# A macaron layer on one core: the first unit's row maxima moved ahead, and the first batch's stores shared by two DMA queues

## The chip, the cores and the metric

The kernel runs on one core of a Trainium2 chip. The metric is device time in microseconds (us), the median of three runs. A core has five engines that each work through their own instructions in order: TensorE (PE in the profile; PEld is its weight load), VectorE (DVE), ScalarE (ACT), GpSimd (POOL) and SyncE (SP). DMAs are issued by an engine's instruction stream, here by SyncE and ScalarE; a DMA that has to wait for data holds up everything behind it on the engine that issues it. Engines wait for one another by semaphores. PSUM is the memory that TensorE writes to.

## The reference

Half a mixture-of-experts step, causal attention with 16 heads of 16, and the other half step, each on the normalised input and added to it. The shapes are 8 batches of 1024 tokens of 256 values.

```python
x = x + 0.5 * _L0_ffn_ref(_layernorm(x), gate_w, w1, b1, w2, b2)
x = x + _L0_attn_ref(_layernorm(x), Wq, bq, Wkv, bkv, Wo, bo)
x = x + 0.5 * _L0_ffn_ref(_layernorm(x), gate_w, w1, b1, w2, b2)
# in attention
dots = jnp.einsum('bhid,bhjd->bhij', q * scale, k)
dots = jnp.where(causal, MASK_VAL, dots)
out = jnp.einsum('bhij,bhjd->bhid', softmax(dots), v)
# in the feed-forward part: an expert counts only if it got at most `cap` tokens
keep = counts <= cap
valid = keep[a_e]
```

An expert that is chosen by more tokens than its capacity is dropped as a whole. The kernel first computes the gates and the attention as if no expert were kept, counts the choices, and only where an expert is kept after all does it run the code for experts (`tc.If` at the end). With these inputs that code does not run: what is timed is the attention, with both gates.

## The kernel before

**Units.** `attention` works in 32 units, `u` from 0 to 31: 8 batches `b` of 4 groups `g` of 4 heads (NG is 4). For each unit there are two kinds of step, 18 of each.

- *M steps* (`m_steps`): matmuls `sm<-qk` give scores with queries on the partitions, a matmul with `masked` and `before_k` adds the causal mask, and VectorE reduces each PSUM pair to row maxima (`mx<-sm`). `done` is the number of the last step that belongs to the first half of the queries. Then `settle` takes the maximum over pieces, splits its negative into a high and a low part (`mneg`), and turns it (`mside`); `send` writes it to DRAM (`rows<-mside`) and reads it back as rows (`neg<-rows`), once for each half.
- *E steps* (`e_steps`): `sc<-neg,take_m` puts the negative maxima into PSUM, `sc<-qk` adds the scores with keys on the partitions, ScalarE takes the exponential (`pT<-sc`), GpSimd zeroes what lies past the diagonal, and `pav<-pT,vaug` multiplies by the values. An E step needs the maxima of its half.

**Work of a batch**, done in pieces between those steps: `enter` (transposes `pta`, copied to `xnT` by ScalarE), `project(b, gp)` (queries and keys of 8 heads, `pq`), `values_of` (`pv`, copied to `vaug`, with the gate's logits), and later `leave` (output projection `px`, residual, second gate). `project` makes of each 128x512 piece a `whole`, its high part `high` (rounded, by ScalarE) and its low part `low` (by GpSimd), and stores four copies in DRAM (`parts<-high`, `parts<-low`): t = 0 for queries, 1 for keys, c the four copies. `fetch(u)` reads a unit's queries and keys from there (`qk<-parts`) with four DMAs. All of these DMAs are on SyncE's queue.

**Order.** The source's order is kept on each engine (`Lane` ties every instruction to the one before it on its engine). In the main loop `step` runs one M or E step, starts DMAs that are due after a lag counted in steps (`start`, `due`), takes up to `small` pieces of `side` (a queue of VectorE and GpSimd work such as `prepare`, `settle`, `gate_first`, `biased_late`), and every `every` steps takes about `rate` pieces of `work` (a queue of TensorE work). M steps run three ahead of the E steps' unit. Units of the first batch use the same `rate`, 17/12 every 3 steps, as the later ones; `u = -1` runs only the 18 M steps of unit 0.

**The start.** `read(0)` and `read(1)` load two batches; `weights` is a generator (`turning`) that loads and transposes the weights in stages, with `pt_gate`, `pt_w`, `pt_wg`, `pt_b` as its PSUM tiles. `prepare_first` and `normed` normalise batch 0 (`xn_a`), `enter(0)` and `project(0, 0)` follow, half a batch at a time with a `fetch` after each half. Then the rest of `turning`, `values_of(0)`, `prepare(1)` (the statistics and first four tiles of batch 1), memsets, the fetch of unit 1, and the main loop, with `project(0, 1)` as its first work and `biased_late(0)` and `gate_first(0)` in `side`.

Of the kernel before, what the change touches and what calls it, by code (L numbers as in the profile page):

```python
# [10 lines left out]
F32 = mybir.dt.float32  # L11
# [9 lines left out]
P = 128  # L21
# [8 lines left out]
def macaron_kernel(  # L30
# [16 lines left out]
    nc = tc.nc  # L47
# [84 lines left out]
    nc.vector.tensor_copy(take_m, rows.to_broadcast([P, P]))  # L132

    wqT = const.tile([P, DC, D], F32, name="wqT")
    wkT = const.tile([P, DC, D], F32, name="wkT")
# [466 lines left out]
    def attention(run_no, src, dst, gate0, logits, tally):  # L602
# [4 lines left out]
        with stack:  # L607
# [76 lines left out]
            def normed(b, jj):  # L684
                mv, ve, rstd = lns[b]
                for j in (2 * jj, 2 * jj + 1):
                    xn = xns[b, j] = norm.tile([P, D], F32, tag="xn", name=f"xn_a{b}_{j}", bufs=4)
                    ln_apply(xn, xbs[b], j, mv, rstd[:, j : j + 1])
                    yield
                if b:  # L690
                    biased(b, jj)

            coming = {}
# [28 lines left out]
            def prepare_first():  # L722
                st, mv = ln_tiles("a0", "a")
                ve = norm.tile([P, TB], F32, tag="vea", name="ve_a0")
                rstd = norm.tile([P, TB], F32, tag="rstda", name="rstd_a0")
                lns[0] = (mv, ve, rstd)
                for n in (slice(0, TB // 2), slice(TB // 2, TB)):
                    for j in range(TB)[n]:
                        ln_stats(xbs[0], j, st, mv)
                    on.gpsimd.tensor_scalar(ve[:, n], mv[:, n, 1], EPS, None, ALU.add)  # L730
                    on.gpsimd.tensor_tensor(rstd[:, n], ve[:, n], half[:, n], ALU.pow)

            def enter(b):
                xnT = xnTs[b] = ap.tile([P, DC, S], F32, tag="xnT", name=f"xnT{b}", bufs=1)
# [22 lines left out]
            def project(b, gp):  # L757
                xnT = xnTs[b]
                parts = parts_d[b, gp] = passing.tile([2, 8, 4, HD, S], F32, tag=f"parts{gp}", name=f"parts{b}_{gp}")
                for s0 in range(0, S, 512):  # L760
                    for t, (wT, bT, scale) in enumerate(((wqT, bqT, QSCALE), (wkT, bkT, 1.0))):
                        pq = bank(f"pq{b}_{gp}_{s0}_{t}")
                        for o in (0, 256):
                            for c in range(DC):
                                product(
                                    pq[:, o : o + 256],
                                    wT[:, c, gp * P : (gp + 1) * P],
                                    xnT[:, c, s0 + o : s0 + o + 256],
                                    start=(c == 0),
                                    stop=(c == DC - 1),  # L770
                                )
# [12 lines left out]


# [62 lines left out]
            def m_steps(u):  # L848
# [56 lines left out]
                def settle(hf):  # L905
                    mx = ap.tile([P, 4, 2, 2], F32, tag="mxr", name=f"mxr{u}_{hf}")
                    on.vector.tensor_reduce(
                        mx.rearrange("p x b a -> p x a b"),
                        mx_tiles[u % 3][hf].rearrange("p h r (a b) s -> p (h r) a b s", a=2),
                        AX.X,  # L910
                        ALU.max,
                    )
                    yield
                    mx = mx.rearrange("p x b a -> p x (b a)")
                    neg = ap.tile([P, 4, 2, 4], F32R, tag="mneg", name=f"mneg{u}_{hf}")
                    high, low = neg[:, :, 0], neg[:, :, 1]
                    on.vector.tensor_scalar(high, mx, -1.0, None, ALU.mult)
                    yield
                    on.vector.scalar_tensor_tensor(
                        low.bitcast(F32), mx, -1.0, high.bitcast(F32), ALU.mult, ALU.subtract  # L920
                    )
                    yield
                    turned = ap.tile([P, 32], F32, tag="mside", name=f"mside{u}_{hf}")
                    on.vector.transpose(turned, neg.bitcast(F32).rearrange("p x c i -> p (x c i)"))
                    start(send(hf, turned), 0)
                    yield

                def send(hf, turned):
                    rows = passing.tile([8, 512], F32, tag="rows", name=f"rows{u}_{hf}")
                    on.sync.dma_start(out=rows.rearrange("c (i s q) -> s c i q", i=4, s=4), in_=turned)  # L930
                    yield 6
                    for h in range(2):
                        on.sync.dma_start(
                            out=negs[u % 2][hf][64 * h : 64 * h + 2, :, :512].bitcast(F32),
                            in_=rows[4 * h : 4 * h + 4].rearrange("(r c) s -> c r s", c=2),
                        )
# [271 lines left out]
            next(turning, None)  # L1208
            next(turning, None)
            drain(read(1))  # L1210
            for t in (vaugs[0], *mx_tiles[0]):
                on.gpsimd.memset(t, 1.0 if t is vaugs[0] else -3.0e38)
# [7 lines left out]
            for jj in range(2, 4):  # L1220
                drain(normed(0, jj))
            projecting = project(0, 0)
            for _ in range(8):
                next(projecting)
            drain(fetch(0, 0, 512))
            drain(entering)
# [5 lines left out]
            for t in (vaugs[1], *mx_tiles[1], *mx_tiles[2]):  # L1232
                on.gpsimd.memset(t, 1.0 if t is vaugs[1] else -3.0e38)
            for pair_of in negs:
                for t in pair_of:
                    on.gpsimd.memset(t.bitcast(F32), 0.0)
# [48 lines left out]
            def maxima():  # L1285
                v, k = divmod(stream[0], 18)
                if v == NU:
                    return
                if k == 0:
                    units[v] = m_steps(v)  # L1290
                steps, settle, done = units[v]
                steps[k]()
                if k == max(done, 8) or k == 17:
                    side.appendleft(settle(int(k == 17)))
                    urgent[0] = 4
                if k == 17:
                    units.pop(v)
                stream[0] += 1

            for u in range(-1, NU):  # L1300
                b, g = divmod(u, NG)
                rate, every = 17 / 12, FILLS
                if u < 0:
                    pass
                elif g == 0:
                    spare[0] = False
                    if b + 1 < B:
# [1 line left out]
                        if b:  # L1309
                            work.append(mixed(leave(b - 1), project(b + 1, 1)))  # L1310
                        else:
                            work.append(project(b + 1, 1))
                        work.append(values_of(b + 1))
                    if b:
                        start(divide(b - 1, 1, 0), 4)
                        after[u - 1, 1] = divide(b - 1, 1, 1)
                        side.append(gate_first(b))
                elif g == 1 and b + 1 == B:
                    work.append(leave(b - 1))
                elif g == 2:  # L1320
                    if b == 0:
                        start(read(2), 40)
# [107 lines left out]
```

## Time and profile before

| | before |
| --- | --- |
| median of 3 runs | 1207.94 us (1207.55 to 1210.71) |
| profiled execution, own time | 1207.5 us |
| its span in the profile | 1205.5 us |
| mean granted TensorE clock | 0.978 of full |
| VectorE busy with `mx<-sm` | 684.7 us, 576 of 1215 ns |
| ScalarE busy with `pT<-sc` | 573.0 us, 576 of 1022 ns |
| `parts<-high` and `parts<-low` | 128 DMAs each, 256 KB each, all on SyncE's queue |
| `qk<-parts` | 124 DMAs on SyncE's queue |

The profile shows one execution. Its busy times are shares of the whole span; in a kernel of 32 like units a stage that happens once is a small share of each, so the timeline and the chain of waits of that stage have to be read. The chain goes back from a late instruction, at each step to what released it. In the timeline a line is a run of like instructions: start, length, engine, operation, out<-in, count, and in brackets the idle time before it with what ended it. "SPq" and "ACTq" lines are DMA issues of SyncE and ScalarE; their length is that of the issuing, not of the transfer. "issue" as a releaser means that the profile shows no cause. The granted clock is TensorE's, as a share of full speed.

### The profile page before, as it was taken

The page shows a single profiled execution, that of the slowest core. Times are in us where ns is not written, and L with a number is a line of the kernel's source. Part 1 is how long each engine was busy: PE and PEld are TensorE (multiplying, and loading weights), DVE is VectorE, ACT ScalarE, POOL GpSimd, SP SyncE. Part 2 cuts the span into 40 slices and gives each one's busy share as a digit, 9 for nine tenths or more (in the row PEclk, how much of TensorE's full clock was granted, in tenths as well). Part 3 has the DMA queues.
Part 4 walks back from the last instruction along what each step waited for, and adds up shares of the span by engine and source line. Part 5 has one row for each costly group of instructions (what it writes and reads, how often), then busy time and mean ns, then how long its engine had stood idle before and what let it go on. Part 6 is the DMA issues. An engine that isn't in the chain of part 4 may idle for free.

```text
span 1205.5 us, 36314 instructions
## 1 busy us (share of the span) xinstructions
PE 1138.4 (94%) x15178; PEld 663.1 (55%) x15178; DVE 935.2 (78%) x1652; ACT 735.6 (61%) x955; POOL 433.8 (36%) x772
## 2 busy tenths in 40 slices
PE   6789899999999999999999999999999999999983
PEld 4445555655556555655556555565556555555542
DVE  2687558887788877988788877888789888798834
ACT  3236656766666666665666656566666666665671
POOL 4633313543333423532235433333235322232331
PEclk9879999999999999999999999999999999999997
DMA  5644654354554646455563645546564555543211
GB/s 178 222 168 141 209 173 128 111 196 153 171 185 154 198 159 190 143 172 177 157 201 113 207 153 168 169 155 202 160 181 150 176 174 177 155 136 109 63 42 39
DMA packets 108517, 190.25 MB, mean 158 GB/s; under 512 B 24752, under 2 KB 42296, under 8 KB 108344
## 3 DMA queue, kind: packets, MB, share of 16 engines
q1 hardware_dynamic: 104952, 185.59, 47.8%
q8 instruction: 122, 2.00, 0.7%
q10 hardware_dynamic: 3392, 2.24, 0.6%
q14 instruction: 51, 0.42, 0.1%
HBM read 94.50 MB, written 93.31 MB: 156 GB/s over the span
## 4 chain that ended last, share of the span: by engine, by line
PE 76%; DVE 13%; DMA 5%; issue 1%; ACT 1%; POOL 1%; SPq 1%; POOLq 0%; ACTq 0%; DVEq 0%
PE sc L626 22%; PE pav L626 21%; PE sm L626 15%; PE pq L626 8%; DVE mx L626 8%; PE px L626 4%; PE pv L626 4%; PE pta L626 2%; DVE st_a L626 1%; DMA few<-sums 1%; DMA neg<-rows 1%; DMA rows<-mside 1%; SPq L626 1%; DVE mv_a L626 1%; DMA qk<-parts 1%
## 5 line engine op out<-in xcount | busy, mean ns | idle before, releaser
L626 DVE TENSOR_REDUCE mx<-sm 128x2 f32<-128x1024 f32 (+2 forms) x576 | 684.7, 1215 | 161.6 <-PE sm L626 159.9
L626 ACT ACTIVATE pT<-sc 128x1024 f32<-128x1024 f32 x576 | 573.0, 1022 | 309.6 <-PE sc L626 297.9
L626 PE MATMUL pav<-pT,vaug 128*32 128x256 f32 (+3 forms) x4608 | 329.7, 387 | 2.0 <-ACT att L626 1.4
L626 POOL TENSOR_SCALAR_AFFINE_SELECT pT<-pT 128x256 f32<-128x256 f32 (+1 forms) x448 | 191.0, 443 | 297.2 <-ACT pT L626 290.4
L626 PE MATMUL sm<-qk 64*128 64x512 f32 (+3 forms) x1536 | 266.2, 384 | 17.4 <-DVE mx L626 8.4
L626 PE MATMUL sc<-neg,take_m 64*128 64x512 f32 x1152 | 263.7, 454 | 16.6 <-DVE mx L626 8.9
L626 PE MATMUL sc<-qk 64*128 64x512 f32 (+3 forms) x1536 | 228.7, 334 | 0.0
L626 PEld LDWEIGHTS sm<-qk 64*128 64x128 f32 x1536 | 140.7, 187 | 120.4 <-issue 51.9
L626 POOL TENSOR_TENSOR low<-whole,high 128x512 f32<-128x512 f32 x64 | 82.0, 1282 | 311.3 <-ACT high L626 302.5
L626 PEld LDWEIGHTS pav<-pT,vaug 128*32 128x32 f32 x4608 | 113.7, 109 | 108.0 <-issue 52.2
L626 PEld LDWEIGHTS sc<-neg,take_m 64*128 64x128 f32 x1152 | 109.4, 186 | 106.8 <-issue 53.6
L626 PEld LDWEIGHTS sc<-qk 64*128 64x128 f32 x1536 | 146.2, 186 | 16.3
L626 PE MATMUL sm<-masked,before_k 64*128 64x128 bf16 (+1 forms) x1280 | 86.3, 213 | 0.0
L626 PE MATMUL pq<-xnT,wqT 128*32 128x256 f32 x1024 | 76.3, 391 | 0.5 <-ACT xnT L626 0.5
L626 PE MATMUL px<-woT,on 128*32 128x264 f32 x1024 | 76.5, 387 | 0.2 <-ACT on L626 0.2
L626 PE MATMUL pq<-xnT,wkT 128*32 128x256 f32 x1024 | 73.2, 395 | 0.0
L626 PE MATMUL pv<-wvT,xnT 128*32 128x264 f32 x1024 | 72.3, 390 | 0.0
L626 PEld LDWEIGHTS <-before_k 64*128 64x128 bf16 x1280 | 37.9, 96 | 43.1 <-issue 26.6
L626 POOL TENSOR_TENSOR x_a<-x_a,bo_all 128x512 f32<-128x512 f32 x32 | 41.6, 1304 | 28.1 <-DVE xn_a L626 28.1
L626 PEld LDWEIGHTS pq<-xnT,wqT 128*32 128x32 f32 x1024 | 34.0, 112 | 31.8 <-issue 13.9
L626 DVE TENSOR_TENSOR x_a<-px,x_a 128x256 f32<-128x256 f32 x64 | 26.2, 410 | 31.2 <-PE px L626 30.6
L626 PEld LDWEIGHTS px<-woT,on 128*32 128x32 f32 x1024 | 34.7, 110 | 26.6 <-issue 9.8
(131 smaller groups left out, 741.4 us busy)
## 6 DMA issues: line engine op xcount, KB each, us to landing
qk<-parts SPq DMA_DIRECT2D x124, 512.0 KB
parts<-high SPq DMA_DIRECT2D x128, 256.0 KB
parts<-low SPq DMA_DIRECT2D x128, 256.0 KB
sums<-att SPq DMA_DIRECT2D x62, 256.0 KB
out_dram<-x_a SPq DMA_DIRECT2D x16, 512.0 KB
on<-sums SPq DMA_DIRECT2D x30, 256.0 KB
rs<-inv SPq DMA_DIRECT2D x30, 256.0 KB
x_a<-in_L_attn_x_dram SPq DMA_DIRECT2D x13, 512.0 KB
```

Source lines behind the costliest of these rows:

```text
L626: i = call(*args, **kwargs)
```

## The change

Three things change together.

1. *The start is put in another order.* Batch 0 is normalised two tiles at a time as soon as two tiles have their statistics (`some`); the `take_m` cast moves behind it. `fetch(1)` and the statistics of batch 1 come right behind the fetches of unit 0, and `values_of(0)` becomes work of the main loop, ahead of `project(0, 1)`. So the M steps of unit 0 follow the weights directly. The loop at `u = -1` takes work after every step, 16/5 pieces in the first five steps and 16/13 in the others. The first half's maxima of unit 0 are settled right behind the step `done`.
2. *Queues.* In batch 0 ScalarE issues the stores of `high` (but for the first copy of the first half's queries and keys, which SyncE keeps), and for unit 0 also `rows` and `neg`, with other lags. The stores of `low` stay with SyncE.
3. *The first batch's fill.* Units 0 to 3 take 13/12 pieces instead of 17/12, `values_of(1)` and `project(1, 1)` are mixed, `gate_first(0)` and `biased_late(0)` enter `side` in unit 0's turn, and the bias additions of batch 1 come as `biased_late(1)` in unit 1's turn instead of beside its normalisation.

The steps themselves and the number of matmuls, copies and DMAs are as before, and nothing is changed for batches from 2 on.

```diff
@@ prepare_first
-                for n in (slice(0, TB // 2), slice(TB // 2, TB)):
-                    for j in range(TB)[n]:
+                def some(j0, j1):
+                    for j in range(j0, j1):
                         ln_stats(xbs[0], j, st, mv)
+                    n = slice(j0, j1)
                     on.gpsimd.tensor_scalar(ve[:, n], mv[:, n, 1], EPS, None, ALU.add)
                     on.gpsimd.tensor_tensor(rstd[:, n], ve[:, n], half[:, n], ALU.pow)
+                for t in (vaugs[0], *mx_tiles[0]):
+                    on.gpsimd.memset(t, 1.0 if t is vaugs[0] else -3.0e38)
+                some(0, 2)
+                some(2, 4)
+                drain(normed(0, 0))
+                next(turning, None)
+                drain(normed(0, 1))
+                on.vector.tensor_copy(take_m, rows.to_broadcast([P, P]))
+                some(4, 8)
@@ project
-                            on.sync.dma_start(out=parts[t, :, c, :, s0 : s0 + 512], in_=part.bitcast(F32))
+                            queue = on.scalar if part is high and (b or gp or s0 or c) and not b else on.sync
+                            queue.dma_start(out=parts[t, :, c, :, s0 : s0 + 512], in_=part.bitcast(F32))
@@ settle, send
-                    start(send(hf, turned), 0)
+                    start(send(hf, turned), 0 if u else 2)
+                    queue = on.sync if u else on.scalar
-                    on.sync.dma_start(out=rows.rearrange("c (i s q) -> s c i q", i=4, s=4), in_=turned)
-                    yield 6
+                    queue.dma_start(out=rows.rearrange("c (i s q) -> s c i q", i=4, s=4), in_=turned)
+                    yield 6 if u else 4
@@ the start
-            for jj in range(2):
-                drain(normed(0, jj))
-            next(turning, None)
             entering = enter(0)
...
             drain(fetch(0, 512, 512))
+            drain(fetch(1))
+            preparing = prepare(1)
+            for _ in range(TB + 1):
+                next(preparing)
...
             drain(turning)
-            drain(values_of(0))
-            drain(prepare(1))
...
-            drain(fetch(1))
-            work = deque([project(0, 1)])
-            side += [biased_late(0), gate_first(0)]
+            work = deque([values_of(0), project(0, 1)])
+            side.append(preparing)
@@ the main loop
-                if k == max(done, 8) or k == 17:
+                if k == (max(done, 8) if v else done) or k == 17:
-                rate, every = 17 / 12, FILLS
+                rate, every = (17 if b else 13) / 12, FILLS
-                            work.append(project(b + 1, 1))
-                        work.append(values_of(b + 1))
+                            work.append(mixed(values_of(b + 1), project(b + 1, 1)))
+                        if b:
+                            work.append(values_of(b + 1))
-                        side.append(gate_first(b))
+                    side.append(gate_first(b))
+                    if not b:
+                        side.append(biased_late(b))
+                elif g == 1 and b == 0:
+                    side.append(biased_late(1))
-                        step(maxima, 2, 4 if n < 5 else 4 / 3, 1)
+                        step(maxima, 1, 16 / 5 if n < 5 else 16 / 13, 1)
```

More of the change, by code (lines that the diff above doesn't have):

```diff
@@ L131, in macaron_kernel @@
     take_m = const.tile([P, P], F32R, name="take_m")
-    nc.vector.tensor_copy(take_m, rows.to_broadcast([P, P]))
     wqT = const.tile([P, DC, D], F32, name="wqT")
@@ L689, in normed @@
                     yield
-                if b:
+                if b > 1:
                     biased(b, jj)
@@ L924, in settle @@
                     on.vector.transpose(turned, neg.bitcast(F32).rearrange("p x c i -> p (x c i)"))
-                    start(send(hf, turned), 0)
+                    start(send(hf, turned), 0 if u else 2)
                     yield
                 def send(hf, turned):
+                    queue = on.sync if u else on.scalar
                     rows = passing.tile([8, 512], F32, tag="rows", name=f"rows{u}_{hf}")
-                    on.sync.dma_start(out=rows.rearrange("c (i s q) -> s c i q", i=4, s=4), in_=turned)
-                    yield 6
+                    queue.dma_start(out=rows.rearrange("c (i s q) -> s c i q", i=4, s=4), in_=turned)
+                    yield 6 if u else 4
                     for h in range(2):
-                        on.sync.dma_start(
+                        queue.dma_start(
                             out=negs[u % 2][hf][64 * h : 64 * h + 2, :, :512].bitcast(F32),
@@ L1210, in attention @@
             drain(read(1))
-            for t in (vaugs[0], *mx_tiles[0]):
-                on.gpsimd.memset(t, 1.0 if t is vaugs[0] else -3.0e38)
             prepare_first()
-            for jj in range(2):
-                drain(normed(0, jj))
-            next(turning, None)
             entering = enter(0)
@@ L1219, in attention @@
             next(entering)
-            for jj in range(2, 4):
-                drain(normed(0, jj))
             projecting = project(0, 0)
@@ L1225, in attention @@
             drain(fetch(0, 0, 512))
+            for jj in range(2, 4):
+                drain(normed(0, jj))
             drain(entering)
@@ L1228, in attention @@
             drain(fetch(0, 512, 512))
-            drain(turning)
-            drain(values_of(0))
-            drain(prepare(1))
[L1232 to L1236, printed above, removed]
-            drain(fetch(1))
-            work = deque([project(0, 1)])
-            side += [biased_late(0), gate_first(0)]
+            drain(fetch(1))
+            preparing = prepare(1)
+            for _ in range(TB + 1):
+                next(preparing)
+            for k in range(2):
+                for t in negs[k]:
+                    on.gpsimd.memset(t.bitcast(F32), 0.0)
+                for t in mx_tiles[k + 1]:
+                    on.gpsimd.memset(t, -3.0e38)
+            on.gpsimd.memset(vaugs[1], 1.0)
+            drain(turning)
+            work = deque([values_of(0), project(0, 1)])
+            side.append(preparing)
             timed = []
```

## The prediction

> **What bounds the kernel now.** I read the page first. TensorE is busy for 94% of the span, but slices 1, 2 and 6 of 40 (30 us each) have low digits, and so has the last. The change edits only the start and the first batch, so slices 1 to 8 matter.
>
> ```profile
> PE 1138.4 (94%) x15178; PEld 663.1 (55%) x15178; DVE 935.2 (78%) x1652; ACT 735.6 (61%) x955; POOL 433.8 (36%) x772
> PE   6789899999999999999999999999999999999983
> PEclk9879999999999999999999999999999999999997
> ```
>
> Next the chain of waits, from 12 to 78 us: what held back the first score matmul (`sc`, at 76.49). Columns: start, length, what.
>
> ```profile
> 19.68 5.62 DMA parts<-high
> 32.27 7.95 PE pv L626 x128
> 42.22 1.68 POOL rstd_a L626
> 43.92 2.33 DVE xn_a L626 x4
> 46.24 1.14 DVE mx L626
> 71.36 4.99 DMA neg<-rows
> 76.49 0.84 PE sc L626 x4
> ```
>
> All eight value tiles (8 us) run before the first maximum; then VectorE, in order, first normalises batch 1 (`xn_a`, waiting for GpSimd's `rstd_a`). Eighteen maxima of 1.2 us follow, from 46.16 to 72.98, and the row of maxima still has to travel through DRAM (`rows`, `neg`).
>
> Then the timeline of SyncE's queue, one line of TensorE's timeline, and busy times by stretch (columns there: PE, PEld, DVE, ACT, POOL busy, TensorE clock, DMA share, GB/s).
>
> ```profile
> 21.25 2.80 SPq L626 DMA_DIRECT2D parts<-high  x2
> 24.15 2.52 SPq L626 DMA_DIRECT2D parts<-low  x2
> 26.84 6.48 SPq L626 DMA_DIRECT2D qk<-parts  x4
> 42.95 9.33 SPq L626 DMA_DIRECT2D qk<-parts  x8
> 139.27 0.55 SPq L626 DMA_DIRECT2D neg<-rows  x2
> 143.28 1.19 SPq L626 DMA_DIRECT2D qk<-parts  x1
> 152.87 0.80 PE L626 MATMUL sm<-qk 64*128 64x512 f32 x2 [5.75 <-issue]
> ```
>
> ```profile
> 4.00:6.00 2.00, 1.09 (x4) 0.72 (x4) 1.37 (x5) 0.29 (x2) 2.00 (x4) 1.00 1.09 376
> 24.00:26.00 2.00, 0.66 (x4) 0.42 (x4) 0.00 (x0) 1.22 (x4) 0.85 (x1) 1.00 0.52 196
> 62.00:64.00 2.00, 0.80 (x2) 0.29 (x2) 2.00 (x3) 0.47 (x1) 1.27 (x1) 0.50 0.50 170
> 204.00:212.00 8.00, 6.58 (x68) 3.41 (x71) 7.83 (x16) 4.06 (x4) 1.93 (x2) 1.00 0.58 191
> ```
>
> While only SyncE's queue writes `parts`, the DMA engines are half busy (0.52) at 196 GB/s; an issue that took 0.58 us takes 1.2 to 1.4, the time of 256 KB at that rate (1.34). With two queues at work (4 to 6 us) they moved 376 GB/s. At 147 us everything stops for 5.75 us: unit 3's `sm` wants the `qk` issued at 143.28, behind a backlog of writes.
>
> Where the 18 scores of each unit begin, counted off TensorE's timeline: 76.49, 114.44, 154.74, 189.26, 219.40. So units 0 to 3 took 37.95, 40.30, 34.52 and 30.14 us, together 142.9. Unit 3 has no projection work left and waits for maxima (2.1 us) while unit 1 and 2 are crowded. The next batches take 139.5 and 139.1 though they also run `leave`.
>
> **The change, part by part.** *Up to the first maximum.* Tiles 0 to 3 are normalised some 2 us earlier, but ScalarE still issues its loads until 11.43, and its copy moves only from 11.86 to about 11.45: -0.4. Of the batch's 16 high stores 14 go to ScalarE at 0.58 us each. The first two fall where ScalarE idled 0.57 us; the four of the second half put 2.3 us ahead of the weight copies, less the 0.8 us that the fourth `high` waited for a buffer: the last weight copy goes from 26.54 to about 28.2, `pt_b` ends near 34.0 instead of 32.27, and the first `sm` runs there (now 40.09). Its data: six writes instead of eight on SyncE's queue, 2 x 1.34 + 0.5 us earlier, so the last lands near 28.5 instead of 31.7, and the four fetches by 32.5. If ScalarE's issues were stretched like SyncE's to 1.4 us, the start is 37. First maximum at 34.7 instead of 46.16. VectorE does batch 1's 16 statistics (4.6 us, 33.0 to 37.6 now) before, while it waits anyway; were its x late, they cost up to those 4.6.
>
> *The five masked steps.* TensorE now weaves all value tiles in: 8 x 1.00 (7.97 above), plus five `sm` of 0.45 to 0.65 with masks (2.8; the timeline at 40.09 and 42.85), plus about 1.2 while the clock is still half (in the trace it rose 4 us after `pt_b` began): 34.0 + 12 = 46. VectorE needs 6 for its five and idles.
>
> *The other thirteen.* TensorE: 6.2 for the `sm` (eight plain at 0.42, five masked as before), 7.7 for the four projections (1.93 each), 13.9; VectorE: 13 x 1.19 + 0.35 for an `xn`, 15.8. Coupled step by step I take 17, plus 0.8 for settling (0.21 + 0.17 + 0.17 + 0.21 where GpSimd is quiet; the two 1.2 us `mneg` of the trace lie beside GpSimd's bias additions, which move later) and one maximum of the next unit that frees the PSUM pair: 46.4 + 17 + 0.8 + 1.2 = 65.5, say 66. The second half's keys: four low writes end near 36 and four fetches bring them by 41, before 46. So the scores start at 66 instead of 76.49: **-10.5**. Bounds: 62 (VectorE never waits) and 77 (TensorE at half clock, 13.9 x 2 = 27.8 instead of 17).
>
> *The maxima's own DMAs* leave a backlogged queue (rows issued 4.1 us after `mside`). The first half's arrive long before use. For the second, ScalarE itself now waits for `rows` ahead of its second exponential: landing took 4.9 us (77.15 to 82.07) to 7.7 (131.62 to 139.27) behind a backlog; about 4 us of other work lies between, so **+1** (0 to 4). Behind it stand the exponentials, and behind them the PSUM pairs.
>
> *The batch's fill.* 13 items per unit instead of 17, with values and second projection woven, fill unit 3 as well. A full unit takes 34.45 with 17 items (units 5 to 7), so 13 cost four quarter projections less (4 x 0.48): 32.5. Units 1 and 2 at 32.6, unit 3 with 12 items 32.4, unit 0 37.95 - 1.9 = 36: 133.6 instead of 142.9, **-9.3**; as the crowded queue may keep a little, I take **-8**. Against this from the other side: a later batch, 139.3, less `leave` (8 tiles of the shape of `pv`, 8.0), plus the 3.4 that unit 0 loses at its slow start (clock 0.50 from 78 to 80 us, 0.76 to 90), is 134.7. Bounds: -2 (the stall of 5.75 and its cold restart stay) and -10.
>
> *At nothing:* `take_m`, the memsets, bias additions and gate choice of batch 0 (VectorE was 6.3 to 7.5 of 10 us busy in unit 0; GpSimd less). Were VectorE full there, the 15 gate operations of 0.2 us would cost 3.
>
> The profiled execution took 1207.5 (span 1205.5), the median is 1207.94. -10.5 + 1 - 8 = -17.5 gives 1190.4; I say **1190**.
>
> **A rule against it.** "DMA: Bandwidth & Descriptors", Rules for kernel authors, in the Trainium skill: spreading DMAs over several engines doesn't help bandwidth, since all share the same 16 DMA engines. The rows above disagree in part: one queue left half of them idle. By the rule 4 MB of writes and 2 MB of reads go at 196 GB/s from 17.5, the second half's keys come near 49, the scores start 3 us later, and the sum would be 1193.
> "TensorE: Matmul & The Clock Gate", A second HAM failure mode, warns that short idling between PSUM-paced groups swings the clock. No row shows it at 82% busy (204 to 212: clock 1.00). By the rule the thirteen steps take 27.8 and the sum would be 1201.
>
> **Rivals.**
> - *The moved work slows the maxima* (15%): the clock drops to 0.50, as from 57 to 71 us now. For: it was lost when TensorE was half idle (0.90 of 2 us at 54). Against: 82% busy kept it. Scores start at 74, gain 2.5 + 8 - 1: 1198.
> - *SyncE's backlog stays* (10%): batch 1's parts are still on SyncE, with the same four writes ahead of the fourth `qk`. Against: only one group of writes now stands between the fetches, where two did. Gain 10.5 - 1 + 2: 1196.
> - *Slower* (9%): TensorE is at half clock for the whole stretch from 34 us to the first score, and on through unit 0. The stretch holds 8.0 of values, 9.0 of `sm`, 7.7 of projections and 2.6 of the next unit's `sm` and transposes, 27.3 us at full clock, 54.6 at half: scores at 88.6, 12 late; unit 0's 20 us of M and E work at half for another 5 beyond today's: +17 - 8 + 1, 1218. It decides once scores start after 87 (76.5 + 8 - 1 + 3.6). Against: continuous work raised the clock within 5 us (32 to 34, 71).
> - *No change* (6%): part of that, scores at about 85.
>
> **How the numbers follow.** Forecast 60%: 1190, by its own bounds 1184 to 1196. The two middle rivals (25%) lie at 1196 to 1198, so 1182 to 1200 leaves out the last two cases and a little. 0.3% (3.6 us) is about what a measurement of this kernel can tell from no change. Faster: 60 + 25 = 85%; same 6%; slower 9%.
>
> **What would show it.** Right: first maximum at 34 to 35; first `sc` near 66; no stop of 5 us near 147; units 0 to 3 at 36, 33, 33, 32; DMA above 250 GB/s between 20 and 28. Wrong: first `sm` waiting for `qk` past 36; clock 0.5 after 50; ScalarE waiting for `rows`; a gap at the start of unit 2 or 4. The later batches must keep 138 to 142 each; if they change, the forecast is wrong for a reason not in it.

## The result, and the profile after

| | before | after |
| --- | --- | --- |
| median in the comparison | 1206.29 us (6 runs) | 1222.01 us (1219.36 to 1224.23, 6 runs) |
| ratio to before | | 1.0128, 95% interval 1.0101 to 1.0155 |
| profiled execution: span, mean clock | 1205.5 us, 0.978 | 1220.6 us, 0.977 |
| first `sm`; first `sc` | 40.09; 76.49 | 43.49; 74.13 |
| units 0 to 3 | 38.0, 40.3, 34.5, 30.1 | 46.4, 36.4, 32.0, 32.4 |
| start of unit 4 | 219.4 | 221.4 |
| batches 1 to 6 | 839.1 | 849.5 |
| unit 28 to the end | 147.0 | 149.7 |

The change made the kernel slower by 1.3%, where 1190 us had been forecast. A unit is counted, here and below, from the first `sc<-neg` of one unit to that of the next on TensorE's timeline. So 2.0 us of the loss are there when unit 4 starts; 13.1 come later, in batches whose source the change does not touch.

The page's first two parts after the change (busy time by engine, then the busy share in 40 slices):

```profile
PE 1142.4 (94%) x15178; PEld 664.9 (54%) x15178; DVE 935.6 (77%) x1652; ACT 734.7 (60%) x955; POOL 434.3 (36%) x774
PE   5869999999999999999999999999999999999983
PEclk9789999999999999999999999999999999999997
```

The work is the same (15178 matmuls). A slice is 30 us. TensorE lost in slice 1 (6 to 5) and in slice 3, from 60 to 90 us (8 to 6), and won in slice 2 (7 to 8) and slice 5, where the stop at 147 had been (8 to 9).

The chain of waits after, a choice of its pieces between 19 and 90 us (start, length, what):

```profile
19.00 8.28 DMA parts<-low
27.43 7.83 DMA qk<-parts
35.33 0.58 ACTq L625
37.04 1.12 PE pt_w L625 x4
43.56 0.86 PE sm L625 x5
54.58 1.24 DVE mx L625
69.70 9.24 DMA parts<-high
79.01 8.90 DMA rows<-mside
88.61 1.02 ACT pT L625
```

Before, this stretch went over VectorE and SyncE. Now it goes twice from a DMA through a DMA issue of ScalarE (ACTq) to ScalarE's own work. ScalarE's timeline shows what stood in its stream:

```profile
24.65 5.03 ACTq L625 DMA_DIRECT2D parts<-high  x2
29.78 0.69 ACT L625 ACTIVATE whole<-pq,bkT 128x512 f32<-128x512 f32 x1 [5.16 <-DMA parts<-high]
35.33 1.44 ACTq L625 DMA_DIRECT2D parts<-high  x2
36.81 0.17 ACT L625 COPY wvT<-pt_gate 128x16 f32<-128x16 f32 x1 [5.70 <-DMA parts<-high]
79.01 0.54 ACTq L625 DMA_DIRECT2D rows<-mside  x1
79.60 0.59 ACT L625 COPY xnT<-pta 128x512 f32<-128x512 f32 x1 [6.07 <-DMA parts<-high]
87.99 0.57 ACTq L625 DMA_DIRECT2D neg<-rows  x2
88.61 1.02 ACT L625 ACTIVATE pT<-sc 128x1024 f32<-128x1024 f32 x1 [7.35 <-DMA neg<-rows]
```

From the start of one issue of `high` to the end of the next passed 5.03 us, and `whole`, which stands behind them, came after 5.16 us of idling. Two more hold back `wvT` by 5.70, though that copy needs no DMA. Near 80 us `xnT` stands for 6.07 us behind two stores and `rows`, and the second exponential behind the issue of `neg` for 7.35. TensorE's timeline shows these waits arriving (its first two lines and the last), beside the first `sm` and the first `sc`:

```profile
30.52 1.11 PE L625 MATMUL pt_w<-ident,wsb 128*128 128x128 f32 x4 [5.42 <-ACT whole L625]
37.04 1.12 PE L625 MATMUL pt_w<-ident,wsb 128*128 128x128 f32 x4 [5.40 <-ACT wvT L625]
43.49 0.79 PE L625 MATMUL sm<-qk 64*128 64x512 f32 x2
74.13 0.50 PE L625 MATMUL sc<-neg,take_m 64*128 64x512 f32 x2 [0.43 <-DVE mx L625]
81.16 0.80 PE L625 MATMUL sc<-neg,take_m 64*128 64x512 f32 x2 [5.21 <-ACT pT L625]
```

Why does an issue wait at all? In the built program the DMAs of SyncE and ScalarE take eight completion semaphores in turn, whichever of the two issues them, so an issue also waits until the DMA that had its semaphore before has landed. In the chain that is a `qk<-parts` of SyncE's at 27.43, ended at 35.26, which let ScalarE's issue go at 35.33. The other waits were for older stores of ScalarE's own: the second of the two issues from 24.65 on came at 29.09, when the store of 19.95 had landed (29.07), and `rows`, whose data was ready at 72.97, at 79.01, when the store of 69.70 had (78.94). In the trace each of the 14 issues by itself took 0.58 to 1.76 us; the rest of the 5.03 was waiting. `neg` in turn waited until `rows` had landed, 8.90 us after its issue. So ScalarE went at the pace of the stores, those of both queues. "DMA: Bandwidth & Descriptors", Anatomy of one DMA (a section on GpSimd's path), in the Trainium skill, says that a wait for a semaphore happens on the sequencer that issues the DMA, ahead of dispatch; these rows agree.

Busy times by stretch (PE, PEld, DVE, ACT, POOL busy; TensorE clock; DMA share; GB/s):

```profile
4.00:6.00 2.00, 1.09 (x4) 0.72 (x4) 1.53 (x5) 0.48 (x2) 2.00 (x4) 1.00 1.09 370
24.00:26.00 2.00, 1.10 (x22) 0.46 (x10) 0.00 (x0) 0.62 (x1) 1.26 (x1) 1.00 0.52 155
50.00:62.00 12.00, 12.00 (x164) 5.43 (x162) 10.17 (x15) 3.84 (x14) 0.96 (x4) 1.00 0.66 244
64.00:82.00 18.00, 11.95 (x164) 6.07 (x162) 14.24 (x20) 5.58 (x9) 4.59 (x5) 0.93 0.52 178
```

With both queues storing `parts` (24 to 26, 64 to 82) the DMA engines stand at 0.52 and 155 to 178 GB/s, where before one queue had 0.52 and 196; over the same stretch, 20 to 28 us, it is 183 GB/s before and 178 after. From 64 to 82 us the two queues share the rate, 83 GB/s on SyncE's and 94 on ScalarE's. The row at 4 us, which does reach 370, holds loads of weights and of `x`, no stores of `parts`. That the kind of transfer makes the difference, and not the number of queues, could be seen in the kernel before, where SyncE's queue alone moved 401 GB/s while it fetched `qk`:

```profile
54.00:56.00 2.00, 0.90 (x10) 0.19 (x2) 2.00 (x3) 0.26 (x1) 2.00 (x3) 1.00 1.00 401
```

### The profile page after: what moved, and what is told of

It is laid out like the page before. It is cut to its first block, busy times and chain, and to the rows that moved or that the text cites. A ratio compares the mean times of both kernels' runs of the same rounds, so it can differ in the third digit from the quotient of the medians.

```text
span 1220.6 us, 36311 instructions
## 1 busy us (share of the span) xinstructions
PE 1142.4 (94%) x15178; PEld 664.9 (54%) x15178; DVE 935.6 (77%) x1652; ACT 734.7 (60%) x955; POOL 434.3 (36%) x774
## 4 chain that ended last, share of the span: by engine, by line
PE 75%; DMA 10%; DVE 6%; POOL 2%; issue 2%; ACT 2%; SPq 1%; ACTq 1%; POOLq 0%; DVEq 0%
PE sc L625 22%; PE pav L625 21%; PE sm L625 15%; PE pq L625 7%; PE pv L625 5%; PE px L625 4%; DVE mx L625 4%; DMA rows<-mside 3%; PE pta L625 2%; DMA neg<-rows 2%; SPq L625 1%; DMA qk<-parts 1%; DMA inv<-few 1%; DMA parts<-high 1%; ACT pT L625 1%
## 5 line engine op out<-in xcount | busy, mean ns | idle before, releaser
L625 PE MATMUL sc<-neg,take_m 64*128 64x512 f32 x1152 | 266.5, 458 | 18.0 <-ACT pT L625 5.2
L625 PE MATMUL pq<-xnT,wqT 128*32 128x256 f32 x1024 | 74.1, 388 | 3.2 <-ACT xnT L625 3.2
L625 PE MATMUL pv<-wvT,xnT 128*32 128x264 f32 x1024 | 76.0, 394 | 0.0
L625 PEld LDWEIGHTS px<-woT,on 128*32 128x32 f32 x1024 | 34.5, 111 | 27.0 <-issue 10.8
```

The source lines that it names most:

```text
L625: i = call(*args, **kwargs)
```

## The experiments

All runs in one table, times in us; "rest" is from the start of unit 4 to the end of the profiled span, in which all kernels run the same instructions, but for a handful at its edge, and differ at most in where the fill stands. Medians of before lie between 1205.25 and 1206.71, so ratios are compared.

| kernel | first `sc` | units 0 to 3 | unit 4 starts | rest | median | ratio to before (95%) |
| --- | --- | --- | --- | --- | --- | --- |
| before | 76.5 | 38.0 40.3 34.5 30.1 | 219.4 | 986.1 | | 1 |
| after | 74.1 | 46.4 36.4 32.0 32.4 | 221.4 | 999.2 | 1222.01 | 1.0128 (1.0101 to 1.0155) |
| e1_phase | 74.0 | 48.6 36.3 31.9 32.4 | 223.4 | 986.8 | 1216.17 | 1.0113 (1.0063 to 1.0164) |
| e2_sync | 72.4 | 42.5 36.2 32.0 32.5 | 215.4 | 992.7 | 1210.08 | 1.0032 (1.0002 to 1.0061) |
| e3_sync_phase | 69.8 | 42.6 36.5 32.0 32.4 | 213.2 | 988.0 | 1202.65 | 0.9974 (0.9950 to 0.9998) |
| e4_before_phase | 73.8 | 36.4 39.7 35.5 30.1 | 215.6 | 993.0 | 1211.12 | 1.0059 (1.0036 to 1.0082) |
| e5_rows_act | 68.4 | 43.8 35.4 32.0 32.4 | 212.0 | 992.0 | 1202.48 | 0.9971 (0.9952 to 0.9989) |
| e6_high_act | 76.6 | 39.7 36.4 31.9 32.5 | 217.1 | 990.9 | 1205.23 | 1.0004 (0.9974 to 1.0034) |
| e7_bias_late | 71.0 | 39.6 33.0 32.7 32.4 | 208.8 | 989.9 | 1201.64 | 0.9958 (0.9939 to 0.9976) |
| e8_fill_only | 77.9 | 32.9 32.2 32.6 33.0 | 208.6 | 992.7 | 1196.58 | 0.9912 (0.9885 to 0.9939) |
| e9_rows_pool | 71.7 | 37.0 33.4 32.7 32.4 | 207.2 | 986.6 | 1196.91 | 0.9935 (0.9903 to 0.9966) |
| e10_start_only | 71.6 | 43.6 37.2 34.7 32.0 | 219.1 | 990.8 | 1211.86 | 1.0061 (1.0035 to 1.0087) |
| e11_fill_carried | 74.5 | 35.5 32.1 32.7 33.0 | 207.8 | 986.6 | 1197.86 | 0.9937 (0.9918 to 0.9956) |
| e12_rate_only | 74.9 | 35.4 33.2 32.5 33.1 | 209.2 | 987.2 | 1198.68 | 0.9940 (0.9915 to 0.9965) |

Rows with the same start code (before, e4_before_phase, e8, e11, e12) have their first `sc` between 73.8 and 77.9, and the rest of like kernels varies by 6: a single profile settles no difference under 4 us in the start, or under 6 us in the rest.

**1. The queues, and a fraction that is carried on (e1 to e4).** `gap` keeps what it could not spend of `rate` in `behind[0]`. Worked out from the source: before, 0.75 stands there at the start of every unit from 1 on; with the changed rates 0.0833 does (1.0833 at units 4, 8, ...), to the end of the run. So from unit 4 on every piece of fill may stand one step differently, in batches that the diff does not name. e1 sets the old fraction in the changed kernel, e4 the new one in the kernel before; e2 takes the queues back, e3 does both.

```diff
# e1 and e3: after;  e4: before, with 1.0833333333333313
             for u in range(-1, NU):
                 b, g = divmod(u, NG)
+                if u == NG:
+                    behind[0] = 0.75
# e2 and e3
-                            queue = on.scalar if part is high and (b or gp or s0 or c) and not b else on.sync
+                            queue = on.sync
...
-                    queue = on.sync if u else on.scalar
+                    queue = on.sync
```

> The changed kernel, with the fraction of a work piece that is carried from unit to unit (behind) set at the start of unit 4 to the 0.75 that the kernel before carries there (the changed one carries 1.083). From unit 4 on every engine's order is then that of the kernel before. Theory A (the later batches lost 10.5 us and the tail 3.9 because the fill stands elsewhere between the steps): batches 1 to 6 take 139.2 to 142 us each, the tail 55.4, the whole 1222 - 14 = 1208. Rival B (they are slower for a reason that the order does not carry: late transfers, the clock, a state left by batch 0): 1222. Batch 0 and its start stay as in the changed kernel (first scores at 74, unit 0 46 us).

> The changed kernel, with all stores of high and the first unit's rows and neg back on SyncE's queue. Theory A (ScalarE, holding at its own DMA issues, held the weight copies by 9.5 us and the second exponential by 7.4, and the second queue brought no bandwidth): first sm at 34 to 38 instead of 43.5, first scores at 66 to 70 instead of 74.1, unit 0 at 37 to 40 us instead of 46.4, whole 1222 - 12 = 1210, range 1206 to 1213. Rival B (one queue is too slow for the moved order: the second half's keys come late, and the maxima row lands as late as on ScalarE): first scores at 74 or later, whole 1218 to 1224.

> Both edits together. If the two losses are separate they add: 1222 - 14 - 12 = 1196, range 1191 to 1200. If the second queue is what the moved order needs: about 1208, as the carried fraction alone.

> The kernel before, with the carried fraction set at unit 4 to the value that the changed kernel has there; nothing else differs from the kernel before, and from unit 4 on the order is that of the changed kernel. Theory A: later batches and tail lose the 14 us, 1206 + 14 = 1220, range 1215 to 1222. Rival B: 1206.

Taking the queues back is worth 0.96% of the time, some 12 us (1.0128 to 1.0032), and 1.4% where the fraction is 0.75 (1.0113 to 0.9974). First `sm` comes at 34.95 and 34.64 then, instead of 43.49. The fraction is worth less than the 14 us asked of it: e4 is slower than before by 0.59%, some 7 us, and e3 faster than e2 by as much (0.9974 against 1.0032). The third pair, e1 and after, can't tell: 5.8 us in the medians but 1.8 in the ratios, on four runs of e1, with intervals that overlap. e3 fell short of its 1196, and its traces say where. SyncE's timeline in e3:

```profile
73.51 2.56 SPq L625 DMA_DIRECT2D parts<-high  x2
76.17 2.51 SPq L625 DMA_DIRECT2D parts<-low  x2
78.80 1.15 SPq L625 DMA_DIRECT2D rows<-mside  x1
84.22 0.54 SPq L625 DMA_DIRECT2D neg<-rows  x2
```

and lines of TensorE's in e3:

```profile
48.30 0.50 PE L625 MATMUL sm<-qk 64*128 64x512 f32 x2 [0.95 <-DMA qk<-parts]
51.95 0.51 PE L625 MATMUL sm<-qk 64*128 64x512 f32 x2 [2.58 <-DMA qk<-parts]
85.81 1.06 PE L625 MATMUL sc<-neg,take_m 64*128 64x512 f32 x2 [6.20 <-DMA neg<-rows]
```

The second half's keys come near 52, not at 41. And unit 0's second half waits 6.20 us for `neg`, whose `rows` had its data at 68.59 and was issued at 78.80, behind sixteen stores that `project(0, 1)` had put into SyncE's queue from 58 us on.

**2. Which DMAs hurt ScalarE (e5, e6).** Both from e3, the first with unit 0's `rows` and `neg` on ScalarE, the second with the stores of `high`.

```diff
# e5, against e3
-                    queue = on.sync
+                    queue = on.sync if u else on.scalar
# e6, against e3
-                            queue = on.sync
+                            queue = on.scalar if part is high and (b or gp or s0 or c) and not b else on.sync
```

> The changed kernel with the fill's carried fraction at 0.75 from unit 4 on, all stores of parts on SyncE's queue, and unit 0's own two turned-maxima transfers (rows and neg) on ScalarE's queue. Compared with the same kernel that has them on SyncE (1202.65 us). Theory A (the second half's rows stood behind sixteen issues of project(0, 1)'s stores on SyncE, 58 to 78.8): rows of the second half goes out near 72 instead of 78.8, the wait of sc for neg at 85.81 (6.20 us) goes, unit 0 takes 37 to 39 us instead of 42.6, total 1197 to 1200. Theory B (whichever queue issues them, they wait for an older transfer to land, because the next free DMA semaphore is that of a store): unit 0 stays at 42 to 46 us, ScalarE waits for parts at the issue, total 1202 to 1207.

> The changed kernel with the fill's carried fraction at 0.75 from unit 4 on, the high parts of q and k stored by ScalarE's queue as in the change, but unit 0's rows and neg on SyncE. Theory A (it is the stores on ScalarE that hold it, 5 us at whole and at wvT before the first sm and again at xnT near 80): first sm near 43, first sc near 73.5 to 74.5, unit 0 44 to 48 us, total 1207 to 1213. Theory B (it is rows and neg on ScalarE that hold it): total 1200 to 1204, unit 0 at 42 us or less.

ScalarE's timeline in e5:

```profile
69.81 0.54 ACTq L625 DMA_DIRECT2D rows<-mside  x1
76.15 3.18 ACTq L625 DMA_DIRECT2D neg<-rows  x2
79.38 1.02 ACT L625 ACTIVATE pT<-sc 128x1024 f32<-128x1024 f32 x1 [7.33 <-DMA parts<-high]
```

`rows` does go out 9 us earlier (69.81 against 78.80), but then ScalarE stands for 7.33 us at the issue of `neg`, until a store of SyncE's has landed; unit 0 takes 43.8, and the total stays (0.9971 against 0.9974). Theory B held. e6 gave neither of its numbers quite: the first `sc` is late (76.6; first `sm` at 45.65), as its theory A has it, but unit 0 takes 39.7 instead of 44 to 48, and the total of 1205.23 lies between the two. So the stores on ScalarE are what delays the start, and together with `rows` and `neg` there they cost most: unit 1 starts at 112.4 in e3, 112.2 in e5, 116.3 in e6 and 122.6 in e1, which has both.

**3. The bias additions (e7).** From e3, with `biased_late(0)` and `biased_late(1)` moved from units 0 and 1 to units 2 and 3.

```diff
-                    if not b:
-                        side.append(biased_late(b))
...
-                elif g == 1 and b == 0:
-                    side.append(biased_late(1))
                 elif g == 2:
                     if b == 0:
                         start(read(2), 40)
+                        side.append(biased_late(0))
...
+                    if b == 0:
+                        side.append(biased_late(1))
```

> The changed kernel with all stores, rows and neg on SyncE's queue and the carried fraction at 0.75, and the additions of the bias of batches 0 and 1 (eight of 1.3 us on GpSimd) moved from units 0 and 1 to units 2 and 3. Theory A (GpSimd, busy without a gap from 110 to 126, delays the casts and with them unit 1): unit 1 takes 32.5 to 34 us instead of 36.5, unit 2 or 3 at most 1 us more, total 1199 to 1201. Theory B (unit 1 waits for something else, the casts of neg or the fetch): unit 1 stays at 36 to 37, total 1202 to 1204.

Busy times from 110 to 126 us, first e3, then e7 (columns as above; GpSimd is the fifth):

```profile
110.00:126.00 16.00, 13.73 (x174) 7.58 (x172) 11.33 (x12) 9.02 (x11) 15.77 (x21) 1.00 0.35 103
```

```profile
110.00:126.00 16.00, 16.00 (x227) 9.40 (x220) 11.59 (x15) 11.66 (x14) 6.73 (x12) 1.00 0.54 156
```

In e3 GpSimd is full (15.77 of 16) and TensorE is not; without the additions TensorE is. Unit 1 takes 33.0 instead of 36.5. The total gained 1.0 in the medians, and the intervals of the two overlap: shown in the stage, not by itself in the total.

**4. The fill alone, and what the early start was worth (e8, e10).** e8 has the kernel before with part 3 of the change alone, without its bias and gate moves; e10 the changed start alone, on SyncE, with the old rate and order of work and the bias additions late as in e7. Both have the fraction 0.75 at unit 4.

```diff
# e8, against before
+                if u == NG:
+                    behind[0] = 0.75
-                rate, every = 17 / 12, FILLS
+                rate, every = (17 if b else 13) / 12, FILLS
-                            work.append(project(b + 1, 1))
-                        work.append(values_of(b + 1))
+                            work.append(mixed(values_of(b + 1), project(b + 1, 1)))
+                        if b:
+                            work.append(values_of(b + 1))
# e10, against e7
-                rate, every = (17 if b else 13) / 12, FILLS
+                rate, every = 17 / 12, FILLS
-                            work.append(mixed(values_of(b + 1), project(b + 1, 1)))
-                        if b:
-                            work.append(values_of(b + 1))
+                            work.append(project(b + 1, 1))
+                        work.append(values_of(b + 1))
```

> The kernel before with one part of the change alone: batch 0's fill at 13/12 with values_of(1) and project(1, 1) mixed (values_of(0) still drained ahead of the units), and the carried fraction set to 0.75 at unit 4, start and queues as before. Theory A (the lower rate takes the stall at 147 away and spares four units one step in three of their fill): first sc at 76.5 as before, batch 0 (38.0, 40.3, 34.5, 30.1 = 142.9 us before) takes 134 to 138, total 1199 to 1203. Theory B (the work is only put off, and comes out in unit 3 and batch 1): batch 0 at 141 to 143, total 1205 to 1208.

> The start of the change alone: its order of the first unit's preparation, all stores on SyncE's queue, batch 0's fill at 17/12 as before, the bias additions late and the carried fraction 0.75 at unit 4. Theory A (the earlier first scores are worth little, since the second half's neg comes at 85.5 whatever the start): first sc at 71, unit 0 at 40 to 42 us, units 0 to 3 together 142 to 148, unit 4 at 213 to 219 (before: 219.4), total 1201 to 1206. Theory B (the start brings its 5.5 to 6.7 us, and it is the lower fill that hides it): unit 4 at 211 or earlier, total 1197 to 1200.

e8 has the lowest median of all, on five runs, with an interval that overlaps those of e9, e11 and e12: units 0 to 3 take 130.7 instead of 142.9, and the total is 0.88% lower. e10 has its first `sc` at 71.6 and starts unit 4 at 219.1, where before has 219.4: theory A, the early start is given back within the batch. Its total of 1211.86 is above even that theory's range; up to unit 4 nothing explains this. In the profile the rest (990.8 against 986.1, with the same instructions) is within the scatter, but the interval of the total is clear of 1. So a kernel with the fraction at 0.75 can lose some 7 us too; that part stays open.

Why it is given back shows where e7 and e8 meet. They start their scores 6.9 us apart and both start unit 1 at 110.6 to 110.8. SyncE's timeline in e7, with a line of TensorE's:

```profile
75.03 2.44 SPq L625 DMA_DIRECT2D parts<-low  x2
77.58 1.18 SPq L625 DMA_DIRECT2D rows<-mside  x1
84.22 0.54 SPq L625 DMA_DIRECT2D neg<-rows  x2
```

```profile
85.84 0.98 PE L625 MATMUL sc<-neg,take_m 64*128 64x512 f32 x2 [4.96 <-DMA neg<-rows]
```

and SyncE's in e8:

```profile
78.47 1.27 SPq L626 DMA_DIRECT2D rows<-mside  x1
83.76 0.55 SPq L626 DMA_DIRECT2D neg<-rows  x2
```

The second half's `rows` had their data at 69.86 and 75.45 but leave at 77.58 and 78.47, `neg` at 84.22 and 83.76: nearly the same time, whenever the scores began. e7 waits 4.96 us for it, and e10 5.22; e8 comes to its second half only then (its first such `sc` is at 87.68) and does not wait.

**5. The second half's rows past the stores (e9).** If that is the limit, it should give way when these three DMAs leave SyncE for GpSimd.

```diff
# against e7
-                    queue = on.sync
+                    queue = on.gpsimd if u == 0 and hf else on.sync
```

> The kernel of e7_bias_late (all stores on SyncE, carried fraction 0.75 from unit 4, bias additions in units 2 and 3), with the second half's three transfers of unit 0's turned maxima (one of rows, two of neg) issued by GpSimd instead of SyncE. In e7 that half's mside is ready at 69.85 and rows is issued at 77.58, behind sixteen stores of project(0, 1); neg lands near 85.5 and TensorE waits 4.96 us for it; e8_fill_only, which starts its scores 6.9 us later, gets the same neg at the same time (rows at 78.47). Theory A (these transfers behind the stores are what takes the earlier start away): rows is issued near 70, neg lands by 79, the wait of 4.96 us goes, unit 0 takes 34 to 36 us instead of 39.6, unit 4 starts at 203 to 206 instead of 208.9, total 1196 to 1199. Theory B (they wait for the stores to land wherever they are issued, or GpSimd is held by its issues): unit 0 stays above 38 us, unit 4 at 208 or later, total 1200 to 1205.

GpSimd's timeline and a line of TensorE's, in e9:

```profile
72.20 0.91 POOL L625 DMA_DIRECT2D rows<-mside  x1
78.53 1.13 POOL L625 DMA_DIRECT2D neg<-rows  x2 [4.51 <-DMA rows<-mside]
84.06 0.39 POOL L625 CAST neg<-neg 66x256 fp32r<-66x256 f32 x1 [1.92 <-DMA neg<-rows]
```

```profile
83.88 0.60 PE L625 MATMUL sc<-neg,take_m 64*128 64x512 f32 x2 [1.38 <-DVE mx L625]
```

`rows` leaves 5.4 us earlier, the wait of 4.96 is gone, and the total of 1196.91 is where theory A has it, though the intervals of e9 and e7 overlap and unit 4 starts only 1.6 us earlier. In e9 these three DMAs also complete on semaphores of their own, outside the eight, so the run doesn't tell the other queue from the other semaphores; e5, which kept the eight and was held at `neg`, points to the semaphores. By the stage theory A is half right: unit 0 takes 37.0 (34 to 36 expected) and unit 4 starts at 207.2 (203 to 206), since TensorE is still 1.38 behind the maxima there and stood 4.0 us for the second half's `qk` before its first `sc`. This is the changed kernel with its queues, its bias additions and its fraction mended, 0.65% faster than before, and no faster than e8, which leaves the start alone.

**6. How little of part 3 it takes (e11, e12).** e11 is e8 without the line for `behind[0]`; e12 is the kernel before with one number changed.

```diff
# e11, against e8
-                if u == NG:
-                    behind[0] = 0.75
# e12, against before
-                rate, every = 17 / 12, FILLS
+                rate, every = (17 if b else 13) / 12, FILLS
```

> The kernel of e8_fill_only (batch 0's fill at 13/12, start and queues as before) without the line that sets the carried fraction to 0.75 at unit 4, so that the fill of the later batches stands one step differently, as in the change. Theory A (the carried fraction costs 5 to 7 us, as e1_phase and e4_before_phase have it): unit 4 starts at 208 to 209 as in e8, batches 1 to 6 together and the tail take 5 to 7 us more than there, total 1201 to 1205. Theory B (the carried fraction costs nothing by itself, and those differences are scatter of the batches): total 1195 to 1199.

> The kernel before with one number changed: batch 0's fill at 13/12 instead of 17/12; values_of(1) stays behind project(1, 1), start and queues as before, and the carried fraction comes out at 0.4167, as in e11_fill_carried. Theory A (the lower rate alone spreads the projections' stores and keeps fill for unit 3, so that no fetch stands behind a backlog): units 0 to 3 at 33 to 36, 32 to 33, 32 to 33, 32 to 33, no stop of 5 us near 147, unit 4 starts at 208 to 211, total 1196 to 1200. Theory B (it takes the weaving of values and second projection as well, since four store groups in a row still stand ahead of unit 3's fetch): a wait of sm for qk or of the fetch of 3 us or more in units 2 or 3, unit 4 at 212 to 216, total 1201 to 1205.

e11 went by theory B. But the fraction that it carries on is a third one, worked out as 0.4167, and not the change's 0.0833: where the fill stands, and not that the fraction changed, decides. 0.75 and 0.4167 are alike in the totals, 0.0833 costs some 7 us in two pairs (e4 and before, e2 and e3). Which collision makes it dearer was not found, and e10 lost as much without it. e12 went by theory A: the rate alone gives the whole gain (0.9940 against 0.9937 in e11), and the weaving of values and second projection adds nothing that shows.

## Why the prediction was wrong, by its own steps

- **First `sm` at 34.0** (measured 43.5): the step that failed first. It charged ScalarE 0.58 us for a store, 1.4 at the worst, "ahead of the weight copies". What was missing is that an issue waits for an older DMA, SyncE's among them, and that everything behind it on ScalarE waits too. The issues themselves took 0.58 to 0.82 us there; the waits in front of them, 3.85 us before 29.09 and 4.2 before 35.33, were not in the sum, and two waits of 5.4 us reached TensorE. The bound of 37 "if stretched" allowed for longer issues, not for waits. With the stores back on SyncE the first `sm` came at 34.6 to 35.0 (e2, e3), close to the forecast.
- **Its data at 28.5, the second half's keys at 41**: two queues were to move more. The stores went at 155 to 183 GB/s between 22 and 26 us, no faster than one queue's had (196), and the prediction's own sign "above 250 GB/s between 20 and 28" failed. The row of 376 GB/s that spoke for it was of loads. The fetches of the second half's keys were issued from 45.24 to 50.51, no earlier than before (42.95 to 49.80). The rule that was weighed against it held for these stores; the 1193 worked out from it was still far too low, as it prices lost bandwidth and not a held engine.
- **From the first `sm` to the first `sc`**: forecast 32 (34 to 66), measured 30.6 (43.5 to 74.1). The five steps took 12.9 us for 12 forecast, the value tiles were woven in, and the clock stayed at 1.00 from 50 to 62 and at 0.93 from 64 to 82. The two rivals that feared for the clock fell. But that the sum agrees is partly luck: the first `sm` came so late that the second half's keys were there. In e2 and e3, with the first `sm` on time, the same stretch took 37.4 and 35.1 us, as TensorE waited for these keys (3.5 us in e3).
- **The maxima's own DMAs, +1 (0 to 4)**: 7.35 for `pT` and 6.07 for `xnT`. That ScalarE would wait for `rows` was foreseen, and too small: `rows` took 8.90 us to land, where 4.9 to 7.7 had been taken. Its own issue came 6.04 us after its data was ready, behind stores on ScalarE that waited for older ones; that was not in the sum. Unit 0 took 46.4, not 36.
- **The fill, -8 (-2 to -10)**: the mechanism was right, and so was the size as far as profiles tell: -12.2 for units 0 to 3 in e8, -9.6 in e11, -8.6 in e12. The stop of 5.75 us is gone (the low digit that stands for it is that of the fifth slice, not the sixth), and units 2 and 3 took 32.0 and 32.4 for 32.6 and 32.4 forecast.
- **-10.5 and -8 were summed, and don't add.** With the queues back, the first `sc` comes 4 to 7 us earlier than before (e2, e3, e7, e9, e10), and that buys nothing by unit 4 (e10), or 1.4 us beside the lower fill (e9 against e8), less than profiles tell apart. In e7 and e10 the second half's `neg`, which comes near 85 by another path, is a limit; with that wait gone (e9) little more was gained, so it is not the only one, and the others were not all found. The step took unit 0 to begin early and go on as ever.
- **Bias additions at nothing**: 3.5 us in unit 1, where GpSimd, the cover that was named, was full.
- **The later batches keep their time**: 849.5 instead of 839.1. The prediction held that this would make it wrong for a reason not in it, and so it did; the carried fraction is that reason for some 7 us of the 13.1, by e4 and e3. Another part of the loss goes with the queues: from e2 to after the rest grows by 6.5, which is hardly more than the scatter. Its place was not found.
- **Slower** had been seen only as a TensorE at half clock. The slower side came about through a ScalarE held at its DMA issues.

In sum: 17.5 us were to be gained. The queues cost some 12 and the fraction some 7. Of the rest, which is e3, 3 us of gain were left (0.9974), as the early start buys next to nothing and the bias additions take back part of the fill's gain.

## What to carry to other kernels

Before a DMA is moved to the queue of an engine that computes, ask what its issue may wait for, an older transfer of another queue included, and what stands behind it on that engine; here an issue of 0.58 us stood behind waits of 4 us. An earlier start is worth no more than the next input on another path allows, here for one the second half's maxima. And where a planner carries a remainder over, a change of rate in one stage moves the work of all later ones: of this change, the one number 13/12 alone, with a remainder that did no harm, made the kernel 0.6% faster.

## What the runs showed of the hardware

- Stores of `parts` from two queues went at the pace of one: DMA share 0.52 in both cases, 155 to 183 GB/s with two and 196 with one, while one queue fetching `qk` moved 401.
- Of the pairs of store issues shown above, one held ScalarE for 1.44 us and one for 5.03, though a single issue took 0.58 to 1.76; compute instructions behind DMA issues waited up to 7.35 us. On GpSimd the issues of three small transfers took 0.91 and 1.13 us in all, and its wait of 4.51 us was for its own `rows`, not for a store.
- With the same instructions in nine kernels, batches 1 to 7 took 986 to 993 us from one profile to the next at a fraction of 0.75; the intervals here leave differences of some 3 us open.
